# Two transformer-like layers on one core: scan steps paced by VectorE's time, bias rows added in their own group, double-buffered statistics, three bands for image 2

## The chip, the cores and the metric

The kernel runs on one core of one Trainium2 chip, in one launch. The metric is device time in microseconds (us), the median of several executions. The core's engines are TensorE (PE, with its weight loads as PEld), VectorE (DVE), ScalarE (ACT), GpSimd (POOL) and the DMA-issuing SyncE (SP). [...]

## The reference, cut to what matters

Two layers over `x` of 2 x 56 x 56 tokens with 384 channels, all in float32:

```python
# layer 0: attention over 7x7 neighbourhoods, then an MLP
x = x + neighborhood_attention(layer_norm(x)) @ w_proj + b_proj
x = x + gelu(layer_norm(x) @ w1 + b1) @ w2 + b2            # 384 -> 1536 -> 384
# layer 1: depthwise 3x3 convolution, scans in four directions, then an MLP
p = layernorm(x) @ w_in + b_in                             # 384 -> 768
local = depthwise_conv3x3(p)
mixed = 0.25 * (lr + rl + tb + bt) + local                 # scans y[t] = 0.6 y[t-1] + 0.4 local[t]
x = x + layernorm(mixed) @ w_out + b_out                   # 768 -> 384
x = x + gelu(layernorm(x) @ w1 + b1) @ w2 + b2
```

## The kernel before, in words

The 6272 tokens are 49 tiles of 128. After the attention (to about 665 us) the first MLP and the projection to `p` run in 13 groups: `groups` is one tile, then twelve groups of four tiles. For a group `g` TensorE makes the 12 blocks of the hidden layer (`m` = 0 to 11, 3 matmuls of 512 columns each, `columns` L1197), then projects the group before into `p` (`project_in`, 6 blocks), then makes the MLP's outputs (`tokens`, four tiles of 24 matmuls of 384 columns). Groups 1 to 4 (`EARLY`) do both matrix products by blocks with seven products in place of eight (`hidden_by_seven` L1616 to L1663, `tokens_by_seven` L1705 to L1751); there VectorE and ScalarE add partial results, and a PSUM bank (`uz`, two of them) is free for TensorE again when VectorE's L1635 or L1663 has read it. From group 6 on, an output bank is seeded first: ScalarE copies the residual `x` into it (`seeded`, L1225), two tiles of it at m = 8 and 10 of the same group, and TensorE accumulates on top. There are three banks (`mm`) for hidden blocks.

The second MLP runs over `dgroups`, twelve groups of four tiles and one of one. Its first three groups (`switch = 3`) still have scan work beside them; from the fourth on it uses seven products again (from about 1935 us). Between hidden layer and outputs of one group stands `project_out` of the next (L1481).

**What runs ahead.** The residual's row of biases (`b2` of layer 0) is added by a DMA of GpSimd with accumulation, straight into `x` (`add_row`, L1136). `add_row` for the next group stands at m = 11; it must wait until ScalarE has read that `x` for its normalized copy (L257, at m = 7 or 8 and on). LayerNorm statistics of tiles 21 to 48 are made ahead, during groups 2 to 4: `statistics_ahead` is a generator that is called at every odd m, loads two tiles from `x1` (384 KB, tile `ahead`, one buffer), and at the next call has VectorE make their statistics (L1551). The statistics of a group's last output tile and their closing (`close_by_pool`, a power on GpSimd, L238) stand at m = 1 of the group after.

**The scans beside.** Convolution and scans run on VectorE beside TensorE's work, from group 5's projection on, over 6 blocks of channels and two images. An image is cut into bands of rows (`BANDS`); a `Band` loads rows of `p` (`pt`), does eight taps on VectorE (L1304; the ninth is ScalarE's or VectorE's `centre`), writes `loc` to two places in DRAM (L1312), does the two scans along the rows (L1250, L1254) into `both`, has ScalarE scale them (L1319), and has GpSimd add them into `mix_d` by DMA (L1323). After an image's bands, a `Columns` job for each channel block does the scans along the columns, with ScalarE turning the data (L1352). A band can begin when its rows and one more have been projected.

`Beside` decides in what place of VectorE's order this work stands. Each step of a job yields its cost on VectorE by formula. After each piece of TensorE's work, `go(worth, own)` adds `rate * worth - own` to what is due and issues steps until it is used up; `worth` is TensorE's time (2.6 for a hidden block, 3.9 for a tile of `project_out`, 7.8 for a tile of outputs), `own` what VectorE does for the main chain meanwhile. `later(issue, steps)` holds an instruction of another engine (the writes, the scaling, the accumulation) back for so many steps:

```python
for entry in self.late:
    entry[0] -= 1
due = [x for x in self.late if x[0] < 0 or got is None]
```

`until(name)` issues all steps up to a job's end at once, and then all that is held back. It stands at the start of group 12 (`last`; image 1's columns must be done, `load_mix(0)` then loads `mx` for the second half) and in the third of the `dgroups` (image 2's). In group 12, `measure_beside` transposes `mx` on TensorE for its statistics (L1440), block `k` of four at m = 2k + 3.

Of the kernel before, what the change touches and what calls it, by code (L numbers as in the profile page):

```python
# [33 lines left out]
F32 = mybir.dt.float32  # L34
# [6 lines left out]
B, H, W, C = 2, 56, 56, 384  # L41
# [20 lines left out]
DECAY, GAIN = 0.6, 0.4  # L62
BANDS = (
    ((0, 28), (28, 47), (47, 56)),
    ((0, 18), (18, 36), (36, 45), (45, 56)),
)
HALF = H // 2
QUARTER = 14
# [45 lines left out]
class Beside:  # L114
# [2 lines left out]

    def __init__(self):
        self.jobs, self.due, self.finished, self.idle = [], 0.0, set(), True
        self.late, self.rate, self.begun = [], 1.07, False  # L120
        self.steps = self.run()

    def behind(self, kind=object):
# [3 lines left out]
        self.jobs[0].load()  # L127
        return self.jobs[0]

    def later(self, issue, steps=1):  # L130

        self.late.append([steps, issue])

    def step(self):
        got = next(self.steps)
        for entry in self.late:
            entry[0] -= 1
        due = [x for x in self.late if x[0] < 0 or got is None]
        self.late = [x for x in self.late if x not in due]
        for _, issue in due:  # L140
            issue()
        return got
# [36 lines left out]
def block_kernel(ctx: ExitStack, tc: tile.TileContext, ins: dict, out: bass.AP):  # L179
# [914 lines left out]
    def passes(xs, xn, w1, w2, between=lambda ps: None):  # L1094
# [142 lines left out]
        def flat(t):  # L1237
            return t.rearrange("p a b -> p (a b)")
# [20 lines left out]
        class Band:  # L1259
# [31 lines left out]
            def steps(self):  # L1291
                beside.behind(Band)
                if self.loc is None:
                    self.centre(nc.vector)
                    yield us(self.n)
                loc, pt = self.loc, self.pt
                for dy in (-1, 0, 1):
                    for dx in (-1, 0, 1):
                        if dy == 0 and dx == 0:
                            continue  # L1300
                        lo, hi = max(self.lo, -dy), min(self.hi, H - max(0, dy))
                        xs, xt, n = max(0, -dx), max(0, dx), W - abs(dx)
                        to = loc[:, lo - self.lo : hi - self.lo, xs : xs + n]
                        nc.vector.scalar_tensor_tensor(  # L1304
                            to, pt[:, lo + dy - self.top : hi + dy - self.top, xt : xt + n],
                            self.tap(dy, dx), to, ALU.mult, ALU.add,
                        )
                        yield us(self.n)
                at = slice(self.lo * W, self.hi * W)
                loc = loc[:, : self.n]  # L1310
                for to in (loc_d, mix_d):
                    beside.later(lambda to=to: nc.sync.dma_start(  # L1312
                        out=to[self.b][self.m, :, at], in_=flat(loc)), 4)
                both = half("both", "out", 4)[:, : self.n]
                behind = beside.behind()
                yield from both_ways(both, loc)
                if isinstance(behind, Band):
                    behind.centre()
                beside.later(lambda: nc.scalar.mul(flat(both), flat(both), share), 8)  # L1319
                beside.later(lambda: add_to_mix(self.b, self.m, at, both), 11)  # L1320

        def add_to_mix(b, m, at, src):
            nc.gpsimd.dma_start(out=mix_d[b][m, :, at], in_=flat(src), accum_op=ALU.add)  # L1323
# [1 line left out]
        class Columns:  # L1325
# [32 lines left out]
            def steps(self):  # L1358
                if not self.lines:

                    self.turn(nc.vector.tensor_copy)
                    yield 2.5
                mixed, behind = [], None

                def turn_back(c, h):
                    if not mixed:
                        mixed.extend(half("mixed", "out", 4) for h in range(2))
                    for i in range(0, HALF, QUARTER):
                        at = slice(c * HALF + i, c * HALF + i + QUARTER)
                        nc.scalar.mul(  # L1370
                            mixed[h][:, :, at].rearrange("p h w -> p w h"),
                            self.lines[c][:, i : i + QUARTER, h * HALF : (h + 1) * HALF], share,
                        )

                for c in range(2):
                    t = self.lines[c]
                    for step, took in enumerate(both_ways(t, t)):
                        if self.b == 0 and c == step == 0:
                            for h in range(2):
                                mixed.append(half("mixed", "out", 4))  # L1380
                                nc.sync.dma_start(out=flat(mixed[h]), in_=self.rows(mix_d, h))
                        if self.b == 1 and c == 0 and step == 1:
                            self.turn(nc.scalar.copy)
                        yield took
                        if c == 1 and step == 0:
                            behind = beside.behind()
                    for h in range(2):
                        if self.b == 0:
                            to = mixed[h][:, :, c * HALF : (c + 1) * HALF]
                            nc.vector.scalar_tensor_tensor(  # L1390
                                to, t[:, :, h * HALF : (h + 1) * HALF]
                                .rearrange("p w h -> p h w"), share, to, ALU.mult, ALU.add,
                            )
                            if c == 0:
                                self.turn(nc.scalar.copy, (h,))
                            elif h == 1 and isinstance(behind, Columns):
                                behind.turn(nc.scalar.copy, (0,))
                            yield us(HALF / 2, 2.0)
                        else:
                            beside.later(lambda c=c, h=h: turn_back(c, h), 1 + c)  # L1400
                    if c == 0:
                        beside.behind()
                if isinstance(behind, Columns):
                    behind.turn(nc.scalar.copy, (1,) if behind.lines else (0, 1))
                if isinstance(behind, Band):
                    behind.centre()
                for h in range(2):
                    if self.b == 0:
                        beside.later(lambda h=h: nc.sync.dma_start(
                            out=self.rows(mix_d, h), in_=flat(mixed[h])), 3)  # L1410
                    else:
                        at = slice(h * HALF * W, (h + 1) * HALF * W)
                        beside.later(
                            lambda h=h, at=at: add_to_mix(self.b, self.m, at, mixed[h]), 4
                        )


# [43 lines left out]
        def measure_beside(m, g, ahead):  # L1461


            n = dgroups[g][1]
            k = m // 2 - 1
            if m == 4:
                add_row(ahead[1], n, "b_out")
            if m == 10:
                ahead[2].close(n)
            if m % 2 == 1 and 0 <= k < n:  # L1470
                measure(ahead[0], ahead[2], k)
                return 2 * STATS
            return 0.0
# [65 lines left out]

        def statistics_ahead():  # L1540

            for k in range(0, n_ready, 2):
                t = tp.tile([P, 2, C], F32, name="ahead")
                at = (ready_from + k) * P
                nc.sync.dma_start(
                    out=t, in_=x1f[at : at + 2 * P, :].rearrange("(k p) c -> p k c", p=P)
                )
                yield
                for i in range(2):
                    st = sm.tile([P, 2, 6], F32, name="st")  # L1550
                    nc.vector.bn_stats(st[:, 0, :], t[:, i, :])  # L1551
                    nc.vector.bn_aggr(ready_mv[:, k + i, :], st[:, :1, :])
            nc.vector.tensor_scalar(ready_rs, ready_mv[:, :, 1], EPS, 1.0, ALU.add, ALU.mult)
            nc.gpsimd.tensor_tensor(
                ready_rs, ready_rs, mhalf[:, :1].to_broadcast([P, n_ready]), ALU.pow
# [128 lines left out]
        def tokens_by_seven(low, high, s1, s2, w2, w2_sums, src, dst):  # L1684
# [7 lines left out]
            t1, t2, t3, t4 = w2_sums  # L1692
            bank_a = ps_y.tile([P, C], F32, name="y").rearrange("p (t c) -> p t c", t=2)
            bank_z = y_end.rearrange("p (t c) -> p t c", t=2)
            u1, u2 = (tp.tile([P, 2, hc], F32, name=x) for x in ("u1", "u2"))

            def of(tiles, half):
                return lambda c, p: tiles[c // 2][:, c % 2, half * 2 * P + p * P : half * 2 * P + (p + 1) * P]
# [75 lines left out]
        for g, (t0, n) in enumerate(groups):  # L1774
# [19 lines left out]
            if g == last:  # L1794
                beside.until((0, NI - 1))
                load_row(0, "b2_1")
                ahead = load_mix(0)
                beside.rate = 1.0
            if g < last:
                x_next, n_next = xs.pop(g + 1), groups[g + 1][1]  # L1800
                norm_next = Norm(sm) if g < EARLY.stop else Ready(g + 1)
# [22 lines left out]
            def behind(m):  # L1824

                nonlocal xn_next
                if g < last:
# [9 lines left out]
                        xn_next = xp.tile([P, NT, C], F32, name="xn")  # L1837
                    if to <= m < to + n_next:
                        norm_next.apply_by_scalar(m - to, x_next, xn_next)
                    if m == NHID - 1:  # L1840
                        add_row(x_next, n_next, "b2_0")

            def both():
                for m in range(NHID):
# [31 lines left out]
            else:  # L1876
# [15 lines left out]
                if waiting is not None:  # L1892
                    project_in(waiting[0], hT_w)
            if g == last:
                w1, w2_1, w_parts = weights(1)
                for part in w_parts[:3]:
                    part()
# [247 lines left out]
```

## Time and profile before

| | |
|---|---|
| median of 3 runs | 2593.45 us (2591.1 to 2599.94) |
| the profiled execution | 2590.42 us, its span 2588.6 us |
| granted TensorE clock, mean | 0.994 |
| VectorE at 1100 to 1200 us | busy 98.32 of 100 us |
| GpSimd in `add_row`, waiting for ScalarE | 130.6 us, 10 waits |
| rows of biases, issue to landing | 6.7 / 8.3 / 19.6 us (min, median, max of 26) |

The profile's page gives busy times and waits of one profiled execution. A wait is given as "engine, tile and line that waited <- what ended the wait". In a timeline, a row is: start in us, duration in us, engine, line, operation, output<-input, shape, and in brackets the idle time of the engine just before and what ended it. Start-to-start times of matmuls are steady in this trace (0.43 us for 512 columns, 0.32 for 384, 0.216 for 256), and so stops of TensorE can be seen one by one.

### The profile page before, as it was taken

Reading aid. Unit: us, or ns where it says so; the run is one execution under the profiler, and the core shown is the slowest. Engines: PE = TensorE matmul, PEld = TensorE weight load, DVE = VectorE, ACT = ScalarE, POOL = GpSimd, SP = SyncE. Lnnn points to the kernel's source line nnn. Section 1 sums busy time; section 2 is a strip of 40 time slices with the busy share of each in tenths; the row PEclk is TensorE's granted clock in tenths of the full one; section 3 lists DMA queues with packets and bytes.
Section 4 is the critical chain, followed back from the end, with each engine's and each line's share of the span. In section 5 each row is a group of like instructions: output and inputs, shape, how many; then the busy total and the mean of one; then the engine's idle time right before and its main releaser. Section 6 shows DMA issues by size and latency. Waiting matters only on the chain. (4 is left out here: it accounts for less than half of the span.)

```text
span 2588.6 us, 42020 instructions
## 1 busy us (share of the span) xinstructions
PE 2538.1 (98%) x16676; PEld 1736.5 (67%) x16678; DVE 1993.0 (77%) x3783; ACT 1127.4 (44%) x2046; POOL 566.9 (22%) x621
## 2 busy tenths in 40 slices
PE   9999999999999999999999998999999999999999
PEld 5666666666787878455445554555558888888888
DVE  4888978887454453899998998989888777878861
ACT  5665655655442344344444443333762333333222
POOL 0111211111532331001110011011123333333332
PEclk9999999999999999999999999999999999999999
DMA  7423454225422222568658676877781333333210
GB/s 229 153 85 99 159 183 148 82 94 199 131 71 64 80 74 63 156 183 212 188 168 309 203 203 172 258 185 182 201 196 39 74 74 74 74 74 74 47 28 21
DMA packets 159058, 343.35 MB, mean 133 GB/s; under 512 B 11543, under 2 KB 112385, under 8 KB 156545
## 3 DMA queue, kind: packets, MB, share of 16 engines
q1 hardware_dynamic: 126688, 256.00, 29.4%
q0 software_dynamic: 27216, 57.81, 13.3%
q10 hardware_dynamic: 4944, 26.74, 3.0%
q8 instruction: 133, 2.18, 0.4%
q14 instruction: 77, 0.62, 0.1%
HBM read 176.73 MB, written 134.88 MB: 120 GB/s over the span
## 5 line engine op out<-in xcount | busy, mean ns | idle before, releaser
L1304 DVE SCALAR_TENSOR_TENSOR loc<-pt,taps,loc 128x495 f32<-128x495 f32 (+12 forms) x336 | 377.1, 1122 | 24.7 <-ACT loc L1287 15.3
L1197 PE MATMUL mm<-hT,w 128*128 128x512 f32 x720 | 320.1, 599 | 3.7 <-ACT hid L1208 3.5
L573 ACT ACTIVATE pts<-pts 119x448 f32<-119x448 f32 (+5 forms) x396 | 210.8, 573 | 106.9 <-DVE pts L563 102.3
L563 DVE TENSOR_TENSOR pts<-sc,bias 119x448 f32<-119x448 f32 (+5 forms) x396 | 219.3, 616 | 45.7 <-PE sc L552 45.4
L1197 PEld LDWEIGHTS mm<-hT,w 128*128 128x128 f32 x720 | 135.9, 192 | 166.4 <-issue 155.9
L1180 DVE STREAM_TRANSPOSE hT<-xn 32x96 f32<-32x96 f32 x784 | 211.2, 269 | 27.7 <-ACT xn L257 17.5
L406 PE MATMUL ps<-hT,wqkv 128*128 128x448 f32 x504 | 204.8, 550 | 2.1 <-ACT vs L451 1.5
L1452 DVE STREAM_TRANSPOSE turned<-mx 32x192 f32<-32x192 f32 x528 | 194.7, 369 | 10.5 <-issue 3.6
L1215 PE MATMUL y<-w,hid 128*128 128x384 f32 x552 | 183.7, 490 | 2.1 <-ACT y L1225 2.1
L1215 PE MATMUL y_end<-w,hid 128*128 128x384 f32 x552 | 181.8, 486 | 0.0
L1215 PEld LDWEIGHTS y<-w,hid 128*128 128x128 f32 x552 | 105.0, 191 | 75.0 <-ACT y L1225 2.7
L1215 PEld LDWEIGHTS y_end<-w,hid 128*128 128x128 f32 x552 | 104.5, 190 | 71.8
L406 PEld LDWEIGHTS ps<-hT,wqkv 128*128 128x128 f32 x504 | 91.3, 189 | 84.4 <-issue 74.2
L1208 ACT ACTIVATE hid<-mm,chan 128x512 f32<-128x512 f32 x120 | 82.0, 687 | 150.2 <-PE mm L1197 150.2
L1197 PE MATMUL mm<-hT,w_in 128*128 128x512 f32 x324 | 140.8, 593 | 0.6 <-DVE hid_u L1635 0.6
L229 POOL TENSOR_TENSOR rs<-rs,mhalf 128x4 f32<-128x4 f32 (+4 forms) x60 | 56.7, 945 | 348.5 <-DVE rs L226 339.5
L1616 PE MATMUL ua<-hT,w 128*128 128x256 f32 x504 | 123.1, 380 | 0.0
L552 PEld LDWEIGHTS sc<-qT,kT 32*100 32x100 f32 (+3 forms) x3168 | 87.9, 169 | 46.7 <-DVE sum L582 7.6
L1623 ACT ACTIVATE hid<-hid_u,chan 128x256 f32<-128x256 f32 x168 | 76.1, 500 | 96.7 <-DVE hid_u L1635 71.8
L592 PE MATMUL o<-pts,vt 100*32 100x112 f32 (+3 forms) x3168 | 115.9, 263 | 0.4 <-ACT pts L573 0.4
L1197 PEld LDWEIGHTS mm<-hT,w_in 128*128 128x128 f32 x324 | 61.3, 190 | 78.1 <-issue 70.8
L552 PE MATMUL sc<-qT,kT 32*100 32x112 f32 (+3 forms) x3168 | 106.7, 269 | 3.4 <-DVE pts L563 3.4
(203 smaller groups left out, 4916.2 us busy)
## 6 DMA issues: line engine op xcount, KB each, us to landing
loc<-loc_d SPq DMA_DIRECT2D x24, 784.0 KB
xa<-x_d SPq DMA_DIRECT2D x24, 768.0 KB
xa<-rows POOLq DMA_DIRECT2D x24, 768.0 KB, 8.6
bias<-in_bias_t ACTq DMA_DIRECT2D x13, 1344.0 KB
p_d<-mx SPq DMA_DIRECT2D x11, 1536.0 KB
mx<-mix_d SPq DMA_DIRECT2D x11, 1536.0 KB
v_d<-vs SPq DMA_DIRECT2D x49, 192.0 KB
xr<-in_x SPq DMA_DIRECT2D x49, 192.0 KB
```

What stands on the lines that cost most here:

```text
L406: nc.tensor.matmul(ps, lhsT=wqkv[:, c, m * P : (m + 1) * P], rhs=hT[:, c, half_of(n)], start=c == 0, stop=c == NC - 1,)
L552: nc.tensor.matmul(sc[i // 2][: w.keys, i % 2, q : q + TT], lhsT=kT[d, hg, w.keys_at + r * w.kc : w.keys_at + (r + w.rows) * w.kc], rhs=qT ...
L563: nc.vector.tensor_tensor(self.pts[:n, h : h + 2, lo:hi, :], sc[half][:n, :, at * TT : (at + hi - lo) * TT].rearrange("p h (c q) -> p h c ...
L573: nc.scalar.activation(t, t, AF.Exp)
L592: nc.tensor.matmul(o[i * HD : (i + 1) * HD, self.slot, :TT], lhsT=w.vt[:n, c, h * HD : (h + 1) * HD], rhs=self.pts[:n, i, c, :], start=c = ...
L1180: nc.vector.transpose(hT[j : j + HD, :, k * P + i : k * P + i + HD], xn[i : i + HD, k, :].rearrange("p (c q) -> p c q", c=NC)[:, :, j : j ...
L1197: nc.tensor.matmul(ps[:, : n * P], lhsT=w[:, c, m * P : (m + 1) * P], rhs=hT[:, c, : n * P], start=c == 0, stop=c == NC - 1,)
L1208: nc.scalar.activation(t[:, : n * P], ps[:, : n * P], AF.Gelu, bias=col(b1, m))
L1215: nc.tensor.matmul(ps, lhsT=t[:, k * P : (k + 1) * P], rhs=w[:, m, :], start=m == 0 and onto is None, stop=m == len(lhs) - 1, skip_group_c ...
L1304: nc.vector.scalar_tensor_tensor(to, pt[:, lo + dy - self.top : hi + dy - self.top, xt : xt + n], self.tap(dy, dx), to, ALU.mult, ALU.add,)
L1452: nc.vector.transpose(t[j : j + HD].rearrange("p (m c) -> p m c", m=NI)[:, :, i : i + HD], mx[i : i + HD, :, k * P + j : k * P + j + HD],)
L1616: nc.tensor.matmul(bank[:, i, :], lhsT=w[:, m * P : (m + 1) * P], rhs=x, start=start and i == 0, stop=True, skip_group_check=True,)
```

## The change

- `later` counts VectorE's estimated microseconds, not steps; an entry is due when its time is used up, seen before the next step's cost is taken off. The numbers at its seven places are changed to match.
- `rate` is 1.03 throughout; it was 1.07, and 1.0 from group 12 on.
- `add_row` of the first MLP stands at m = 2 of the group whose `x` it is, not at m = 11 of the group before. In the last group it comes after the load of `b2` of layer 1 into the same row of `rows`.
- `statistics_ahead` has two buffers and one load in flight ahead; `u1` and `u2` of the first MLP's `tokens_by_seven` are put into halves of the output tile `dst`.
- Image 2 has three bands of 27, 18 and 11 rows; it had four of 18, 18, 9 and 11.
- In group 12 the transposes of `measure_beside` come two `m` later, and the closing of their statistics stands after the projection.

```diff
 BANDS = (
     ((0, 28), (28, 47), (47, 56)),
-    ((0, 18), (18, 36), (36, 45), (45, 56)),
+    ((0, 27), (27, 45), (45, 56)),
 )
...
-        self.late, self.rate, self.begun = [], 1.07, False
+        self.late, self.rate, self.begun = [], 1.03, False
...
-    def later(self, issue, steps=1):
-        self.late.append([steps, issue])
+    def later(self, issue, us=0.0):
+        self.late.append([us, issue])
 
     def step(self):
         got = next(self.steps)
+        due = [x for x in self.late if x[0] <= 0.0 or got is None]
+        self.late = [x for x in self.late if x not in due]
         for entry in self.late:
-            entry[0] -= 1
-        due = [x for x in self.late if x[0] < 0 or got is None]
-        self.late = [x for x in self.late if x not in due]
+            entry[0] -= got
...
                     beside.later(lambda to=to: nc.sync.dma_start(
-                        out=to[self.b][self.m, :, at], in_=flat(loc)), 4)
+                        out=to[self.b][self.m, :, at], in_=flat(loc)), 5.0)
...
-                beside.later(lambda: nc.scalar.mul(flat(both), flat(both), share), 8)
-                beside.later(lambda: add_to_mix(self.b, self.m, at, both), 11)
+                beside.later(lambda: nc.scalar.mul(flat(both), flat(both), share), 9.0)
+                beside.later(lambda: add_to_mix(self.b, self.m, at, both), 12.0)
...
-                            beside.later(lambda c=c, h=h: turn_back(c, h), 1 + c)
+                            beside.later(lambda c=c, h=h: turn_back(c, h), 3.0 + 3.5 * c)
...
-                            out=self.rows(mix_d, h), in_=flat(mixed[h])), 3)
+                            out=self.rows(mix_d, h), in_=flat(mixed[h])), 6.0)
...
-                            lambda h=h, at=at: add_to_mix(self.b, self.m, at, mixed[h]), 4
+                            lambda h=h, at=at: add_to_mix(self.b, self.m, at, mixed[h]), 11.0
...
-            k = m // 2 - 1
+            k = m // 2 - (1 if g else 2)
             if m == 4:
                 add_row(ahead[1], n, "b_out")
-            if m == 10:
+            if m == 10 and g:
                 ahead[2].close(n)
...
         def statistics_ahead():
-            for k in range(0, n_ready, 2):
-                t = tp.tile([P, 2, C], F32, name="ahead")
-                at = (ready_from + k) * P
-                nc.sync.dma_start(...)
-                yield
-                for i in range(2):
-                    ...
+            asked = []
+            for k in range(0, n_ready + 4, 2):
+                if k < n_ready:
+                    t = tp.tile([P, 2, C], F32, name="ahead", bufs=2)
+                    at = (ready_from + k) * P
+                    nc.sync.dma_start(...)
+                    asked.append((k, t))
+                if len(asked) == 2 or k >= n_ready:
+                    yield
+                    at, t = asked.pop(0)
+                    for i in range(2):
+                        ...
+                    if not asked:
+                        break
...
-            u1, u2 = (tp.tile([P, 2, hc], F32, name=x) for x in ("u1", "u2"))
+            if src is dst:
+                u1, u2 = (tp.tile([P, 2, hc], F32, name=x) for x in ("u1", "u2"))
+            else:
+                u1, u2 = (dst[:, 2 * i : 2 * i + 2, hc:] for i in range(2))
...
                 ahead = load_mix(0)
-                beside.rate = 1.0
+                beside.rate = 1.03
...
-                    if m == NHID - 1:
-                        add_row(x_next, n_next, "b2_0")
+                if m == 2 and g:
+                    add_row(x, n, "b2_0")
...
             if g == last:
+                ahead[2].close(dgroups[0][1])
                 w1, w2_1, w_parts = weights(1)
```

More of the change, by code (lines that the diff above doesn't have):

```diff
@@ L1540, in statistics_ahead @@
         def statistics_ahead():
-            for k in range(0, n_ready, 2):
-                t = tp.tile([P, 2, C], F32, name="ahead")
-                at = (ready_from + k) * P
-                nc.sync.dma_start(
-                    out=t, in_=x1f[at : at + 2 * P, :].rearrange("(k p) c -> p k c", p=P)
-                )
-                yield
-                for i in range(2):
-                    st = sm.tile([P, 2, 6], F32, name="st")
-                    nc.vector.bn_stats(st[:, 0, :], t[:, i, :])
-                    nc.vector.bn_aggr(ready_mv[:, k + i, :], st[:, :1, :])
+            asked = []
[3 more added lines that the diff above has]
+                    at = (ready_from + k) * P
+                    nc.sync.dma_start(
+                        out=t, in_=x1f[at : at + 2 * P, :].rearrange("(k p) c -> p k c", p=P)
+                    )
+                    asked.append((k, t))
[3 more added lines that the diff above has]
+                    for i in range(2):
+                        st = sm.tile([P, 2, 6], F32, name="st")
+                        nc.vector.bn_stats(st[:, 0, :], t[:, i, :])
+                        nc.vector.bn_aggr(ready_mv[:, at + i, :], st[:, :1, :])
+                    if not asked:
+                        break
             nc.vector.tensor_scalar(ready_rs, ready_mv[:, :, 1], EPS, 1.0, ALU.add, ALU.mult)
```

## The prediction

> **What bounds the kernel now.** I read the busy table, then the stages of 100 us, then TensorE's waits, then the timelines at its largest stops.
>
> ```profile
> PE 2538.1 (98%) x16676; PEld 1736.5 (67%) x16678; DVE 1993.0 (77%) x3783; ACT 1127.4 (44%) x2046; POOL 566.9 (22%) x621
> ```
>
> TensorE (PE) is busy 98% of the span. The change removes no matmul, so all it can win is what lies between matmuls. The stages say where that is (columns: stretch, us, then busy us and count of PE, PEld, DVE, ACT, POOL, then PEclk, DMA share, GB/s):
>
> ```profile
> 800.00:900.00 100.00, 94.36 (x463) 80.60 (x462) 43.59 (x139) 31.99 (x62) 25.29 (x27) 0.97 0.26 79
> 900.00:1000.00 100.00, 94.53 (x447) 79.34 (x446) 41.11 (x124) 36.12 (x69) 33.66 (x33) 0.97 0.22 64
> ...
> 1100.00:1200.00 100.00, 99.94 (x284) 50.63 (x283) 98.32 (x69) 47.06 (x66) 11.47 (x10) 1.00 0.70 191
> ...
> 1500.00:1600.00 100.00, 93.15 (x265) 48.04 (x264) 92.70 (x86) 38.77 (x58) 9.46 (x9) 0.95 0.74 203
> ```
>
> Two regimes. At 800 to 1000 (the groups of the first MLP that are done with seven products in place of eight) VectorE (DVE) is half idle and PE loses 5.5% all the same, which points at one queue blocked by one wait. At 1100 to 1600 (groups 6 to 12, with the scans beside) DVE is full, and PE stops late in the stage. PE's waits name the instructions:
>
> ```profile
> PE uz L1616 <- DVE sh L250: 12.3, 3, 5.6
> PE mm L1197 <- ACT hid L1208: 3.5, 1, 3.5
> ...
> PE xi L1440 <- DMA mx<-mix_d: 3.3, 1, 3.3
> ```
>
> The 12.3 us are stops at 761, 842 and 924 us. VectorE's timeline ahead of the one at 842:
>
> ```profile
> 832.65 0.56 DVE L221 BATCH_NORM_STATS2 st<-xa 128x6 f32<-128x384 f32 x1 [2.96 <-DMA xa<-x_d]
> ...
> 835.53 0.56 DVE L1551 BATCH_NORM_STATS2 st<-ahead 128x6 f32<-128x384 f32 x1
> ...
> 839.89 0.56 DVE L1551 BATCH_NORM_STATS2 st<-ahead 128x6 f32<-128x384 f32 x1 [2.88 <-DMA ahead<-x_d]
> ...
> 841.24 0.66 DVE L1663 TENSOR_TENSOR hid_u<-uz,hid_u 128x512 f32<-128x512 f32 x1
> ```
>
> L1663 empties the bank that PE waits for. It stands behind statistics that wait 2.88 us for the one `ahead` buffer's load; ahead of those, other statistics wait 2.96 us for `xa`. In the scan stage:
>
> ```profile
> 1569.94 1.04 ACT L1319 ACTIVATE both<-both 128x1008 f32<-128x1008 f32 x1 [9.05 <-DVE both L1254]
> ```
>
> ```profile
> 1351.17 1.35 POOL L1136 DMA_DIRECT2D xa<-rows  x1 [15.06 <-ACT xn L257]
> ```
>
> ScalarE (ACT) stood 9.05 us in front of a scan that VectorE had not reached, with GELUs queued behind. GpSimd (POOL) stood 15.06 us in a bias row that must not overwrite `x` before ACT has normalized it, with an accumulate into `mix_d` queued behind; a `mixed` load then came late, DVE idled 8.88 us at 1365, and PE stopped 2.12 us at 1383.
>
> [...] a stop costs more than itself: after 5.4 to 5.6 us of stop the 10 us stretches at 840 and 920 have a clock of 0.66 (3.4 us lost), after 2.12 us the one at 1380 has 0.83 (1.7 lost), after 1.51 us the one at 1340 has 1.00 (none). [...] Here an `ahead` load issued at 836.77 was there at 839.89. [...]
>
> **Part 1, two `ahead` buffers.** No instruction is added; each load is issued one turn (about 4.5 us) earlier, against 3.1 us of landing. DVE's 2.88 us at 839.89 go, so L1663 starts at 838.4 and PE's 5.59 become 2.7. What is late next is the `xa` load, which stays. Clock loss falls from 3.4 to between 0 and 1.7. Gain 4.6 to 6.3, I take 5.4; the stop at 923.5 has the same form (DVE waits 2.84 and 2.83): twice 5.4 = 10.8. In group 2 a stop of 1.1 us at 767.5 (ACT behind L1635, that behind a 2.24 us `ahead` wait) goes too; the 1.27 at 761.9, where no `ahead` wait precedes, stays. **Sum -12**, ends -7 and -14. `u1`, `u2` moved into `dst` pay for the buffer; copies and adds keep their sizes: 0 [...].
>
> **Part 2, pace.** The planner's ledger can be followed by hand. At the start of group 12, PE work since the scans began is worth 514.8 and VectorE's own work 20.2. Before, 1.07 x 514.8 - 20.2 = 531 us of beside work are issued; after, 1.03 x 514.8 - 20.2 = 510. Before, VectorE can't keep up. In the statistics at m = 1 the lag shows in when POOL's power (L238) starts after the group's first matmul: 8.6, 11.4, 16.6, 17.5, 13.7, 15.8 us for groups 7 to 12. The ledger is lower by 5.5, 6.5, 12.4, 16.7, 17, 20 at those groups (0.04 of PE's worth so far, rounded to whole steps), so nothing is left of the backlog, and the floor stays: m = 1 itself begins 2.6 us into the group, and with the statistics in front L238 should start at about +5 to +7. The flush at group 12 then finds a scan nearly done, and ACT waits some 2 us rather than 9. PE's stops are 1.5 (1345), 2.1 with 1.7 of clock (1383), and at 1571 to 1585 3.5 + 3.3 with about 5 of clock: **16.9 in all**.
>
> **Part 3, bias rows in the own group at m = 2.** It takes POOL's wait for ACT (130.6 us in 10 waits) away and adds none: `x` is long normalized. In the built order the row stands right behind the power and shift of m = 1 in every scan group; in the last it also waits for the `b2_1` load into its row. Who waits for it: ACT's seed of a bank at m = 8, 21 us into the group. With the power at +5 to +7, 2.5 us of POOL work and 8.3 us to landing (median of the 26), it is there at +16 to +18. Cost 0; cover 3 to 5 us, and another 7.7 us (three `mm` banks of 2.57 us) before PE feels ACT. The worst landing seen, 19.6, would just use this up.
>
> **Part 4, group 12's measuring later by two m**, its close after the projection: the first transpose moves from m = 3 to 5, 5.2 us later, against a 3.3 us wait for `mx` (counted in part 2). Until the first project_out, some 50 us on, nobody reads the result: 0.
>
> **Part 5, three bands.** Six fewer bands: 48 taps, 12 scans, 6 end fixes. From the shapes (1540 columns 1821 ns, 495 columns 727 ns) a tap has 0.21 us that doesn't scale; scans (1568: 3424, 504: 1208) 0.16; an end 0.2. 10 + 1.9 + 1.2 = 13 us of DVE, 12 ACT operations, 18 SP and 6 POOL transfers. All beside PE: worth 0 directly. In return a band of 27 rows needs more of image 2: the ledger has one pause of 8 us in group 12, when the next bands aren't projected yet, and DVE idles there.
>
> **Part 6, delays in time.** For wide bands the scaling on ACT comes earlier (9 us rather than 8 steps of 1.84 = 14.7); harmless at a lag under 9. Tail: where `until((1, 5))` drains, before leaves 0 and after 3.65 us (a last scan). DVE ended its scans at 1922.5, its sums at 1934.0, PE took the first product at 1934.8, ACT had hT ready at 1928. Cover 3.6 to 6.7 us; if lag adds, up to 5 us of stop: bound 0 to +5, taken **+2**. Rate 1.03 against 1.0 in groups 12 on: DVE stood at 83 to 92% there; 3% more fits, bound 0 to +3, taken +1.
>
> **Sum.** Of the 16.9, I leave 4 for stops in new places: -13. -12 - 13 + 3 = -22 to the profiled 2590.4 (span 2588.6 and 1.8 around it), 2568. The runs' median 2593.45 is 3 higher: **2571**.
>
> **Rivals.** (a) Both regimes gain, as above: 2571, own range 2561 to 2580. For: the ledger fits the lags. Chance 0.60. (b) Only part 1 pays; scan-stage stops move elsewhere, since DVE is at 98% and DMA at 0.7: 2593 - 12 = 2581. Chance 0.20. (c) The change doesn't do what it says: `xa` stays late with the extra loads beside it and eats part 1, scans stay jammed: 2592. Chance 0.09. (d) Slower: the bias row becomes the late one. If DVE's lag stays at 14 to 17, POOL issues it at +20 and it lands at +29, where PE's cover ends; each further us stops PE in each of seven groups. With 5 us over, 7 x 5 = 35, plus 1.7 of clock each, 12: 2593 - 12 + 47 = 2628. It decides from a landing of +29 on. Against: the lag should be 5. Chance 0.11, mostly milder, near 2605.
>
> About 0.3% (7.8 us) is what a measurement can tell from no change. The range 2558 to 2590 holds nearly all of (a) and (b) and a third of (c). Faster: 0.60 + 0.17 + 0.02 = 0.79; same: 0.03 + 0.07 = 0.10; slower 0.11.
>
> **What would show it.** Right: PE at 800 to 1000 loses about 3 us a hundred, no DVE wait for `ahead`; L238 under 8 us into its group; no ACT wait of 9 us at group 12; PE full from 1100 to 1600. Wrong: ACT's seeds (L1225) waiting for `xa<-rows`; PE's clock still 0.66 after 840; a stop at the hand-over past 1900.

## The result, and the profile after

The changed kernel takes 2581.13 us (median of five executions, 2579.16 to 2583.36), against 2593.45 us for the kernel before in the same comparison: ratio 0.9952, 95% interval 0.9933 to 0.997. It is 12 us faster; 22 us were forecast. The profiled execution took 2580.42 us with a span of 2578.6 us.

TensorE's line of the busy table in the profile after:

```profile
PE 2537.1 (98%) x16678; PEld 1737.8 (67%) x16678; DVE 1978.9 (77%) x3718; ACT 1123.9 (44%) x2033; POOL 569.0 (22%) x615
```

TensorE's own work is what it was (2538.1 us before). VectorE has 14 us less (13 were worked out for three bands). The rest must be seen in the stages, kernel after, columns as in the prediction:

```profile
800.00:900.00 100.00, 95.87 (x469) 81.71 (x468) 44.48 (x144) 32.57 (x62) 25.39 (x28) 0.97 0.26 79
900.00:1000.00 100.00, 97.22 (x471) 81.98 (x471) 41.61 (x125) 39.54 (x77) 34.71 (x33) 1.00 0.25 68
1300.00:1400.00 100.00, 99.74 (x282) 51.24 (x281) 92.25 (x80) 48.68 (x76) 7.02 (x7) 1.00 0.76 253
1400.00:1500.00 100.00, 95.59 (x259) 48.47 (x258) 88.97 (x57) 47.44 (x71) 12.37 (x6) 0.97 0.64 208
1500.00:1600.00 100.00, 100.00 (x303) 52.20 (x302) 94.34 (x70) 44.20 (x62) 9.44 (x8) 1.00 0.65 182
1600.00:1700.00 100.00, 96.27 (x290) 51.24 (x289) 80.49 (x84) 33.06 (x46) 10.48 (x11) 1.00 0.83 248
...
1900.00:2000.00 100.00, 95.02 (x427) 75.84 (x426) 82.99 (x183) 39.70 (x71) 33.31 (x33) 0.98 0.38 84
```

Three things are to be seen. The stages at 800 to 1000 are better, though 800:900 still has a clock of 0.97. 1300:1400 and 1500:1600 are full or nearly so, where before had 96.37 and 93.15, with a clock of 0.98 and 0.95. But 1400:1500, which was full before, now has 95.59 at 0.97, and 1600:1700 and 1900:2000 (99.86 and 98.45 before) have gaps that are new. The stage of the largest loss in the kernel before:

```profile
1400.00:1500.00 100.00, 100.00 (x276) 50.10 (x275) 98.29 (x73) 47.43 (x71) 8.38 (x7) 1.00 0.64 213
```

TensorE's waits in the kernel after (us in total, times, longest) name them:

```profile
PE uz L1623 <- DVE sh L250: 7.8, 3, 4.1
PE tp L271 <- ACT xn L257: 4.7, 2, 4.4
...
PE yb L1229 <- ACT hT L274: 2.7, 1, 2.7
PE y L1215 <- DVE xc L1481: 2.6, 1, 2.6
...
PE ub L1623 <- issue: 2.0, 1, 2.0
```

The first is what part 1 left of the old 12.3 us. The second is the stop that ends at 1422 us, the third and the last are the hand-over past 1900 (from the scans to the groups with seven products), the fourth is a stop at 1648. The stops at 1571 to 1585 are gone, and the ScalarE wait of 9.05 us at the start of group 12 is 0.43 us (timeline of ScalarE, kernel after):

```profile
1557.48 1.47 ACT L1319 ACTIVATE both<-both 128x1512 f32<-128x1512 f32 x1 [0.43 <-DVE both L1254]
```

**The stop at 1422.** Group 10 starts at 1389.2 us. GpSimd's timeline, then ScalarE's, then TensorE's, all of the kernel after:

```profile
1400.37 4.14 POOL L238 TENSOR_TENSOR rs<-rs,mhalf 128x4 f32<-128x4 f32 x1 [62.23 <-DVE off L237]
...
1405.28 1.33 POOL L1136 DMA_DIRECT2D xa<-rows  x1
```

```profile
1419.84 0.48 ACT L1225 COPY y<-xa 128x384 f32<-128x384 f32 x1 [6.00 <-DMA xa<-rows]
1420.26 1.61 ACT L1352 COPY line<-loc 128x392 f32<-128x392 f32 x2
```

```profile
1422.40 1.97 PE L271 MATMUL tp<-ident,xn 128*128 128x128 f32 x8 [4.41 <-ACT xn L257]
```

The power starts 11.2 us into the group, because VectorE gets to it late. It takes 4.14 us, the bias row is issued behind it at +16.1, and it lands at about +30.6. ScalarE stands 6.00 us in front of the seed, with the normalized copy for TensorE queued behind (GpSimd had finished the last of its inputs, `sh`, at 1405.34; it starts at 1421.66), and TensorE stops for 4.41 us. Half clock for 6.8 us (1421.1 to 1427.9, by narrow windows of the trace) then costs 3.4 more. The DMA view of the kernel after from 1395 to 1425 us (issue, KB each, us from issue to landing) shows the landing and what went beside it:

```profile
loc<-loc_d SPq DMA_DIRECT2D x2, 784.0 KB
mixed<-mix_d SPq DMA_DIRECT2D x2, 784.0 KB
mix_d<-mixed SPq DMA_DIRECT2D x2, 784.0 KB
xa<-rows POOLq DMA_DIRECT2D x1, 768.0 KB, 14.5
x_d<-xc SPq DMA_DIRECT2D x1, 768.0 KB
```

14.5 us, not 8.3. This is rival (d)'s mechanism, in one group out of seven.

### The profile page after: what moved, and what is told of

The parts are those of the page before. It is cut to its first block, busy times and chain, and to the rows that moved or that the text cites. A ratio compares the mean times of both kernels' runs of the same rounds, so it can differ in the third digit from the quotient of the medians.

```text
span 2578.6 us, 41862 instructions
## 1 busy us (share of the span) xinstructions
PE 2537.1 (98%) x16678; PEld 1737.8 (67%) x16678; DVE 1978.9 (77%) x3718; ACT 1123.9 (44%) x2033; POOL 569.0 (22%) x615
## 5 line engine op out<-in xcount | busy, mean ns | idle before, releaser
L1304 DVE SCALAR_TENSOR_TENSOR loc<-pt,taps,loc 128x1045 f32<-128x1045 f32 (+17 forms) x288 | 366.7, 1273 | 22.0 <-ACT loc L1287 14.2
L1323 POOL DMA_DIRECT2D mix_d<-both x36 | 32.7, 908 | 408.4 <-ACT both L1319 326.2
```

The source lines that it names most:

```text
L1304: nc.vector.scalar_tensor_tensor(to, pt[:, lo + dy - self.top : hi + dy - self.top, xt : xt + n], self.tap(dy, dx), to, ALU.mult, ALU.add,)
```

## The experiments

Each ratio is to the kernel before, run on the same chip; 0.001 is 2.6 us. Differences between two changed kernels below are differences of their ratios.

**1. Part 1 alone** (`b_ahead`): the kernel before, with the two `ahead` buffers and `u1`, `u2` in `dst`.

```diff
-            for k in range(0, n_ready, 2):
-                t = tp.tile([P, 2, C], F32, name="ahead")
+            for k in range(0, n_ready + 4, 2):
+                    t = tp.tile([P, 2, C], F32, name="ahead", bufs=2)
...
```

> The kernel before with part 1 alone (two ahead buffers, u1 and u2 in the output tile). Theory: DVE's waits for ahead vanish in groups 2 to 4, the stops at 842 and 924 shrink from 5.6 and 5.4 to 2.7 to 4 each, and the clock is lost at most once: before minus 5 to 9 us, all of it between 740 and 1000; the scan stage keeps its stops (about 17 us at 1300 to 1600). Rival: with more loads in flight the load of xa comes later by what ahead gained: within 3 us of before.

Measured: 2581.89 us, ratio 0.9965 (0.9957 to 0.9973), or 9 us less. TensorE's stops at 842 and 923 fell from 5.6 and 5.4 us to 2.6 and 2.5, and the clock lost after each from 3.4 to 1.7; all stops of the scan stage stayed. VectorE's timeline ahead of the first, kernel of `b_ahead`:

```profile
830.57 0.56 DVE L221 BATCH_NORM_STATS2 st<-xa 128x6 f32<-128x384 f32 x1 [2.98 <-DMA xa<-x_d]
...
836.19 0.66 DVE L1670 TENSOR_TENSOR hid_u<-uz,hid_u 128x512 f32<-128x512 f32 x1
```

The wait for `ahead` between the two is gone; the one for `xa` is what it was. Part 1 gives about 9 us by itself, so the other parts together gave only about 3.

**2 and 3. The bias row elsewhere.** The changed kernel with `add_row` put back to m = 11 of the group before (`a_bias_back`), and with it in the first step of its own group (`a_bias_m0`):

```diff
-                if m == 2 and g:
+                if m == 0 and g:
                     add_row(x, n, "b2_0")
```

> The kernel after with the bias rows back at m = 11 of the group before. Theory (late row): the stop of 4.4 us at 1422, with 3.4 us of clock, is ACT's seed waiting for the bias row, so it goes; POOL's waits for ACT return (some 100 us), and a mixed load may be late by them, worth at most 3 us of stop: after minus 4 to 8 us. Rival (the row's old place was the harm): POOL blocked in front of the accumulations brings back stops at 1340 to 1390 of 5 us or more: after plus 0 to 6 us.

> The kernel after with the bias row at m = 0 of its own group, ahead of the power of m = 1 on POOL. Theory (late row): POOL issues it 10 us earlier or more in the groups where DVE is behind, ACT's wait of 6.0 us for it in group 10 and the stop at 1422 go: after minus 5 to 8 us, and no ACT wait for the row anywhere. Rival (DMA queues are full at that point whatever the order): the row lands late again or the loads of the columns do, and a stop of 3 us or more stays in group 10: within 3 us of after.

Measured: 2571.23 us, ratio 0.9924 (0.9908 to 0.9939), and 2570.39 us, ratio 0.9921 (0.9905 to 0.9937). Both are 7 to 8 us below the changed kernel by ratio (10 by medians; all their executions took 2566.9 to 2573.3 us, all of the changed kernel 2579.2 to 2583.4), and in both the stop at 1422 is gone and no seed waits for `xa<-rows`. At m = 0 the row stands ahead of the power in GpSimd's queue, so it goes as soon as ScalarE has read `x`, still in the group before. GpSimd's timeline of `a_bias_m0`:

```profile
1398.77 4.14 POOL L238 TENSOR_TENSOR rs<-rs,mhalf 128x4 f32<-128x4 f32 x1 [54.87 <-DVE off L237]
...
1422.60 1.33 POOL L1136 DMA_DIRECT2D xa<-rows  x1 [18.86 <-ACT xn L257]
```

The power is as long and as late as before, but no row is behind it; the row at 1422.60 is the next group's. GpSimd's wait for ScalarE (18.86 us), which part 3 was to remove, is back and costs nothing at this pace. The two kernels differ in where the row is asked for, yet agree; so it is the row's lateness that costs, and not something else about m = 2.

**4. The bias row alone** (`b_bias`): the kernel before with `add_row` at m = 2.

```diff
-                    if m == NHID - 1:
-                        add_row(x_next, n_next, "b2_0")
...
+                if m == 2 and g:
+                    add_row(x, n, "b2_0")
```

> The kernel before with the bias rows of groups 6 to 12 added in the third step of their own group, everything else as before. The theory (the row lies behind the power of L238 in POOL's queue, and now starts when the power is over; in the kernel before the power starts 8.6 to 17.5 us into a group): the row is issued at +12 to +22 us and lands 7 to 15 us later, at +20 to +37, so that at least groups 9 and 10 seed their y late (they need it at about +21, and TensorE stops past +29): TensorE loses 5 to 20 us more than before, ratio 1.002 to 1.008, and ScalarE waits for xa<-rows in two or more groups. Rival 1 (the prediction's step): the move costs nothing at any pace, ratio 1.000 within 0.001. Rival 2: one group alone is late, as in the changed kernel: +4 to +10 us.

Measured: 2591.98 us, ratio 1.0003 (0.9993 to 1.0013): rival 1 by the number, but not by its reason. ScalarE waits for `xa<-rows` three times (6.1 us in all), TensorE's stop of 1.51 us at 1345 has become one of 4.48 us at 1352, and the one at 1579 went from 3.3 to 5.5 us:

```profile
1351.85 2.18 PE L271 MATMUL tp<-ident,xn 128*128 128x128 f32 x9 [4.48 <-ACT xn L257]
```

Against that the old stops at 1383 and 1571 are gone: the first came from GpSimd's blocked queue, and of the 9.05 us for which ScalarE stood ahead of the second, 4.87 are left. At the old pace the move gives about as much as it takes. At the new pace what it gives was to be had without it, and only the taking is left.

**5. The pace alone** (`b_pace`): the kernel before with 1.03 throughout.

```diff
-        self.late, self.rate, self.begun = [], 1.07, False
+        self.late, self.rate, self.begun = [], 1.03, False
...
-                beside.rate = 1.0
+                beside.rate = 1.03
```

> The kernel before with the pace alone changed: 1.03 from the start and after the last group, everything else as before (bias row in the 12th step of the group before, one 'ahead' buffer, four bands). The theory: the stops of the scan stage in the kernel before (about 1345, 1372-1383 and 1561-1585 us, 17 us of excess together) go, the stops in front of L1623 at 760 to 920 us stay, and at the end of image 2 eleven units of VectorE work are left over instead of none, which come back as about 6 to 9 us of stop near 1920 us: 5 to 10 us less than before in sum, ratio 0.996 to 0.998. Rival 1: the stops came from the place of the bias row and not from the pace: they stay, and the leftover adds 5 to 10 us (ratio 1.002 to 1.004). Rival 2: the leftover is hidden by other work: 14 to 17 us less (0.9935 to 0.995).

Measured: 2598.57 us, ratio 1.0026 (1.0019 to 1.0034): 7 us slower. This is rival 1's number, but not by its reason, since the stops did go. The first half of the theory held: 1345, 1383 and the stop behind ScalarE at 1571 are gone. The bill comes in image 2. TensorE's timeline of `b_pace`:

```profile
1572.54 1.51 PE L1440 MATMUL xi<-ident,mx 128*128 128x128 f32 x6 [3.90 <-DMA mx<-mix_d]
...
1854.35 5.07 PE L1197 MATMUL mm<-hT,w 128*128 128x512 f32 x6 [4.68 <-ACT hid L1208]
...
1937.20 0.48 PE L1229 MATMUL yb<-zeros 128*128 128x384 bf16 x1 [5.94 <-ACT hT L274]
1953.33 1.10 PE L1616 MATMUL uz<-xsums,w 128*128 128x256 f32 x4 [4.12 <-DVE hid_u L1663]
```

The two stops past 1900 are the 11 units of VectorE work that a slower pace leaves over (experiments 8 and 9 bear this out). The stop at 1572 (the measuring in group 12) is there at both paces, and the one at 1854 is new. So the pace pays only with something that stands beside it in the change. Experiments 6 to 9 take the measuring, the delays, the bands and the pace at the end one by one; the changed kernel with the old pace throughout wasn't run, so what the pace is worth beside the delays in time stays open.

**6. Measuring put back** (`c_measure_back`, from the kernel of experiment 3):

```diff
-            k = m // 2 - (1 if g else 2)
+            k = m // 2 - 1
...
-            if m == 10 and g:
+            if m == 10:
```

> The kernel with the bias row in the first step of its own group (2570.4 us), with the measuring in group 12 put back: transposes of mx at m = 3, 5, 7, 9 and the closing at m = 10, as in the kernel before. The theory: mx is loaded only at the start of group 12, the first transpose at m = 3 waits for it whatever the pace (3.3 us before, 3.9 us with the pace alone, 5.5 us with the bias row alone), so the stop near 1565 us comes back with 3 to 5.5 us and 1.7 us or more of clock: 4 to 8 us more, ratio to before 0.9935 to 0.995. Rival (the prediction's step, which counted this stop as the pace's gain): no stop there, the time stays within 2 us of 2570 us, ratio 0.992.

Measured: 2572.93 us, ratio 0.9924 (0.9911 to 0.9938). In TensorE's timeline the stop is back:

```profile
1559.23 0.84 PE L1440 MATMUL xi<-ident,mx 128*128 128x128 f32 x6 [3.04 <-DMA mx<-mix_d]
```

It is 3.04 us and lost no clock, which the theory had added. The trace settles that part 4 removes this stop; the times (0.0003 in the ratio, 2.5 us in the medians) are too near to show its worth.

**7. Delays in steps again** (`c_later_steps`, from the kernel of experiment 3):

```diff
-        beside.later(lambda: nc.scalar.mul(flat(both), flat(both), share), 9.0)
-        beside.later(lambda: add_to_mix(self.b, self.m, at, both), 12.0)
+        beside.later(lambda: nc.scalar.mul(flat(both), flat(both), share), 8)
+        beside.later(lambda: add_to_mix(self.b, self.m, at, both), 11)
...
-        beside.later(lambda c=c, h=h: turn_back(c, h), 3.0 + 3.5 * c)
+        beside.later(lambda c=c, h=h: turn_back(c, h), 1 + c)
```

> The kernel with the bias row in the first step of its own group (2570.4 us), with the held-back instructions counted in steps again (4, 8 and 11 for a band, 1 + c, 3 and 4 for columns). The theory: the stop of 4.8 us with 3.4 us of clock at 1854 us in the kernel with the pace alone comes from the columns of image 2 being turned back and added at once, so that ScalarE waits for mix_d<-mixed in front of GELUs; it comes back here: 5 to 9 us more, ratio to before 0.9945 to 0.996. Rival 1 (the prediction's step, delays in time cost and bring nothing): within 2 us of 2570 us, ratio 0.992. Rival 2: the stop at 1854 us is due to four bands for image 2 and their crowding, not to the delays: no stop there with three bands, again 0.992.

Measured: 2585.26 us, ratio 0.9973 (0.996 to 0.9985), 13 us more: more than the theory said, and not where it said. Rival 1 falls, and so does rival 2's time. TensorE's timeline of `c_later_steps`:

```profile
1644.53 2.29 PE L1215 MATMUL y<-w_out,mx 128*128 128x384 f32 x3 [6.57 <-DVE xc L1481]
...
1855.30 0.55 PE L1440 MATMUL xi<-ident,mx 128*128 128x128 f32 x3 [1.32 <-DVE st L221]
...
1939.07 2.04 PE L1623 MATMUL uz<-xsums,w 128*128 128x256 f32 x4 [4.07 <-DVE hid_u L1670]
```

At 1854 there are 1.3 us, not 4.8, so the old delays alone don't make that stop, and rival 2's view of it stands. The large ones are at 1644 (2.42 us in `a_bias_m0`) and 1939, with 3.4 us of clock lost at each. Ahead of the first, VectorE idles longer for the rows of the next band (its timeline, `a_bias_m0`, then `c_later_steps`):

```profile
1613.94 0.74 DVE L1289 TENSOR_SCALAR loc<-pt,taps 128x1008 f32<-128x1008 f32 x1 [6.94 <-DMA pt<-p_d]
```

```profile
1619.41 0.75 DVE L1289 TENSOR_SCALAR loc<-pt,taps 128x1008 f32<-128x1008 f32 x1 [11.09 <-DMA pt<-p_d]
```

By steps, SyncE issues two loads of `pt` back to back from 1606.69 us and then the writes of `loc`, and the first rows are used 12.7 us later; in time, one load of `pt` goes at 1605.35, then the writes, the next load behind them, and the rows are used 8.6 us later. That the second load slows the first one is a guess that wasn't tried by itself, and what brings the stop at 1939 stays open.

**8. Four bands for image 2 in the changed kernel** (`a_four_bands`):

```diff
-    ((0, 27), (27, 45), (45, 56)),
+    ((0, 18), (18, 36), (36, 45), (45, 56)),
```

> The kernel after with image 2's four bands as before. Theory (pause): without the 8 us pause in group 12 the DVE is not idle at 1608 to 1623 and not behind in the project_out at 1640, so the stops at 1648 (2.6) and 1676 (1.2) go; but 13 us more of DVE work leave 11 us to drain at the until of image 2, where after drains 3.7, and the stops at the hand-over (2.7 + 2.0 and 1.7 of clock) grow by 5 to 7: after plus 0 to 4 us. Rival: the bands' 13 us of DVE are worth their time on the path: after plus 8 to 13 us, with stops in groups 10 to 12.

Measured: 2580.81 us, ratio 0.9958 (0.9942 to 0.9974): the same as the changed kernel. Underneath, two things changed places. The stops at 1648 and 1676 (2.57 and 1.16 us) are gone with the pause, and the hand-over has 5.97 and 3.14 us of stops instead of 2.69 and 1.99, as was expected from the 11 units of work that VectorE then has left over. TensorE's timeline of `a_four_bands`:

```profile
1919.33 0.48 PE L1229 MATMUL yb<-zeros 128*128 128x384 bf16 x1 [5.97 <-ACT hT L274]
```

**9. A higher pace at the end alone** (`a_tail_rate`):

```diff
-                beside.rate = 1.03
+                beside.rate = 1.06
```

> The changed kernel with the pace raised from 1.03 to 1.06 after the last group of the stage alone, so that the 3.65 units of VectorE work left over at the end of image 2 are issued beside the product; the pause of 8 in group 12 stays where it is. The theory: the stops at 1922 and 1931 us (5.2 us with the clock) go, the rest stays: 3 to 6 us less than the changed kernel, 2575 to 2578 us against its 2581. Rival: those stops are not the leftover's but VectorE's lateness in general, and move: within 1.5 us of the changed kernel.

Measured: 2584.37 us, ratio 0.9969 (0.9956 to 0.9982), about 4 us slower than the changed kernel, though the two intervals overlap; the theory's gain falls. The hand-over is clean (0.06 us lost at 1900 to 2000), so the leftover was the cause there. But with three bands VectorE runs out of projected rows at the pause, and a higher pace gets there sooner. VectorE's timeline, then TensorE's, of `a_tail_rate`:

```profile
1623.44 0.74 DVE L1289 TENSOR_SCALAR loc<-pt,taps 128x1008 f32<-128x1008 f32 x1 [18.61 <-DMA pt<-p_d]
```

```profile
1650.31 5.49 PE L1215 MATMUL y<-w_out,mx 128*128 128x384 f32 x8 [8.16 <-DVE xc L1481]
```

18.61 us of idleness (6.9 + 7.1 with statistics between, in the changed kernel) become a backlog, and `project_out` waits 8.16 us for VectorE, with 5.1 us of clock. One more stop, of 4.05 us with 1.7 of clock, comes at 1863, again behind VectorE.

**10. Bias row first, four bands, 1.06 at the end** (`v_m0_4_106`), for which the planner's sums have neither pause nor leftover: the edits of experiments 3, 8 and 9 together.

> The changed kernel with three edits: the bias row in the first step of its own group, in POOL's queue ahead of the power; the four bands of before; and the pace 1.06 after the last group. By the planner's own sums there is then neither a pause in group 12 nor work left over at the end. The theory: the stop at 1422 us goes (2570.4 us was measured for that alone), and so do the stops at 1640 to 1676 us (3.9 us) and at 1915 to 1931 us (5 to 7 us with the clock): 2559 to 2564 us, ratio to before 0.988 to 0.990. Rival 1: VectorE's 13 us of added band work make it late elsewhere between 1620 and 1930 us: 2566 to 2572 us, as with the bias row alone. Rival 2: the raised pace brings stops of before's kind back into image 2: above 2572 us.

Measured: 2567.29 us, ratio 0.9903 (0.9885 to 0.9921). In microseconds that is rival 1's range, by the ratio the theory's upper end. By the trace there are two stops of over 0.5 us left in image 2, 1.38 us each, at 1641 and 1873, and the hand-over is nearly clean (0.65 us lost at 1900 to 2000). Four bands and a higher pace, each worth nothing or less by itself, fit together by the trace; the 3 to 5 us that they gain over experiment 3 are not clear of the two intervals.

**11. What part 1 left** (`v_stats_later`): the kernel of experiment 10 with the statistics of the next `x` two steps later in groups 0 to 3.

```diff
-                    if g < EARLY.stop and 2 * m < n_next:
-                        for k in range(2 * m, min(2 * m + 2, n_next)):
+                    if g < EARLY.stop and 0 <= 2 * m - 4 < n_next:
+                        for k in range(2 * m - 4, min(2 * m - 2, n_next)):
                             norm_next.add(k, [x_next[:, k, :]])
-                    if g < EARLY.stop and m == 1:
+                    if g < EARLY.stop and m == 3:
```

> The kernel with the bias row first, four bands and the pace 1.06 (2567.3 us), and the statistics of the next x in groups 0 to 3 at m = 2 and 3, not at m = 0 and 1 (their closing with them, from m = 1 to 3). The theory: after the second 'ahead' buffer the stops in front of L1623 at 761, 842 and 920 us (1.4, 3.8 and 2.5 us, and 1.7 us of clock after each of the last two) are VectorE's statistics waiting up to 4.2 us for the load of xa with L1670 behind them; read two steps (about 5 us) later, xa is there, and 7 to 11 us go: 2556 to 2560 us, ratio to before 0.986 to 0.988. Rival: xa is late by nature of the buffer that it goes into, and the statistics or the shift behind them stop TensorE at a later m instead: 2564 to 2570 us, ratio 0.989 to 0.991.

Measured: 2558.15 us, ratio 0.9861 (0.9843 to 0.988), 9 to 11 us less than experiment 10 and within the theory's range. TensorE's waits and its timeline at the old stop at 842:

```profile
PE uz L1623 <- DVE sh L250: 3.8, 3, 1.4
```

```profile
836.60 1.10 PE L1623 MATMUL uz<-xsums,w 128*128 128x256 f32 x4 [1.41 <-DVE sh L250]
```

No clock is lost at 800 to 1000 any more. This version beats both kernels.

## Why the prediction was right or wrong

The time came out 10 us above the forecast and within its range, and the change is faster, as was held likeliest. It is also rival (b)'s number to the microsecond, but its reason, a full VectorE and DMA that move the stops elsewhere, fits only in part: stops did come in new places, 7.8 us at 1422, 3.7 at 1648 and 1676 and 5 at the hand-over with the clock counted, where the working had left 4 for stops in new places and 2 + 1 for the end. But moving one row alone takes the first of these away (experiments 2 and 3). The sum of -22 had one step that was wrong in its mechanism, part 3, and in the other parts gains and costs that were put in the wrong place. All three of the prediction's signs of being wrong showed: a seed that waits for `xa<-rows`, a clock of 0.66 at 840 to 850, a stop past 1900.

**Part 1 (-12 forecast): right, at the low end.** Alone it measured -9, within the ends of -7 and -14. The stops at 842 and 923 became 2.63 and 2.47 us, as worked out (2.7), the one at 767 went and the one at 761 stayed. But 1.7 us of clock was lost after each of the first two, the worse end of "between 0 and 1.7". In the profile of the changed kernel the stop at 842 is larger, 4.09 us with 3.4 of clock, because there VectorE had `xa` 6.0 us after the issue of its load, against 4.6 in the kernel before and in `b_ahead`:

```profile
835.35 0.56 DVE L221 BATCH_NORM_STATS2 st<-xa 128x6 f32<-128x384 f32 x1 [4.43 <-DMA xa<-x_d]
```

This size isn't shown to be the change's: `a_bias_m0` and `c_later_steps` are the same program up to there, and their loads took 5.8 and 4.6 us in the same count. "No DVE wait for `ahead`" held only ahead of L1670; four waits of 4.5 us in all remain. Experiment 11 shows that most of the rest is `xa`'s.

**Part 2 (-13): right for the old stops, wrong on whose they were.** All of the stops from 1345 to 1585 went. But pace alone (experiment 5) does not remove the one at 1579, which is part 4's (3.04 us without clock in experiment 6), and pace alone makes the kernel slower. Counting part 4's 3.3 us "in part 2" hid that. The backlog didn't vanish entirely either: the power starts at 7.2, 6.8, 9.1, 8.2, 11.2, 5.9 and 5.5 us into groups 6 to 12, not at +5 to +7.

**Part 3 (cost 0): the step that failed.** It measured +7 to +8 us by ratio. The arrival of +16 to +18 was made of a power at +5 to +7, 2.5 us of GpSimd work and the median landing of 8.3; in group 10 these were 11.2, 4.9 and 14.5, and the sum 30.6. Each term was taken near its middle, though the row must be in time in all seven groups. The worst landing was looked at, but with the other terms left at their middle: 14.5 us by itself would have been in time. The room of about 11 us up to +29 was less than the three overruns together (4 to 6, 2.4 and 6.2 us). TensorE stopped at +28.8, as the cover of +29 says, but the row's own deadline lay earlier, near +26: from the start of the seed to TensorE's next instruction ScalarE needed another 2.6 us for the seed, two copies of `line` and the normalized copy. So the row was 4.4 us late, not 1.6, and with 3.4 us of clock this makes the 7.8 us that experiments 2 and 3 give back. Rival (d)'s mechanism was seen but tied to a lag of 14 to 17 in every group; one bad group was enough to take more than a third of the gain.

**Part 4 (0):** -3 by the trace, in group 12, as said under part 2; the times can't show it.

**Part 5 (worth 0, with one pause):** the sum is right (experiment 8), the parts are not 0. The pause stops TensorE for 2.57 and 1.16 us, and the shorter work spares 4.4 us of stops at the hand-over, before clock.

**Part 6 (+2 and +1):** the hand-over has 2.69 and 1.99 us of stop and 1.7 of clock, where before had one stop of 1.07: +5, the upper bound. The delays in time were called harmless; at the new pace they are one of the main gains. Taking them back costs 13 us (experiment 7). Nothing in the working priced what the old delays did at the new pace.

With the row in time the same change measures -20 (experiments 2 and 3): the forecast of rival (a) within 2 us. That is partly luck, as a part 1 too large, a measuring and delays that were given no worth of their own and a hand-over too small cancel.

## What to carry to other kernels

An instruction moved next to its reader must arrive in its worst case, not in its median: add up the largest values seen for each term of its path, look at what stands ahead of it in its queue, and count what its reader's engine still has to do before the bottleneck gets its input. When work is paced beside an engine, less pace doesn't remove work but puts it at the end, so pace, band sizes and delays have to be tried together; one alone may well read slower. Where two waits stand in a row on one queue, removing one leaves the other (the stop of 5.59 us became 2.63 in experiment 1), and one trace doesn't fix its size: the same load took 4.6 us in one profile of the same program part and 5.8 in another.

## What the runs showed of the hardware

The clock's loss after a stop is not fixed by the stop's length: 3.04 us ahead of 1559 lost nothing (experiment 6), while 2.12 us ahead of 1383 in the kernel before lost 1.7. In the changed kernel half clock began at 840.83, 1421.10 and 1922.86 us, in the stops of 4.09 and 4.41 us and 0.4 us behind the one of 2.69 us, and lasted 6.8, 6.8 and 3.4 us, which lost 3.4, 3.4 and 1.7; its stops of 2.46 us at 920 and 2.57 us at 1648 lost nothing. What decides it was not shown.

A bias row of 768 KB added to `xa` landed after 6.7 us at best and 14.5 us at worst in the changed kernel (what set the difference wasn't tried); and the power on 128x4 elements took from 1.03 to 4.14 us over its seven groups, as the profile has it. Both spreads belong to the same instruction with the same shape, and no row of medians shows them.
